# Third tiles at full width, an expert's number kept in a register, and another order of ScalarE's copies

## The chip, the cores and the metric

The kernel runs on one core of a Trainium2 chip. The metric is the device time of one execution in microseconds. Five engines run side by side, each taking its own instructions in order: TensorE (PE in the rows, PEld for its weight loads), VectorE (DVE), ScalarE (ACT), GpSimd (POOL) and SyncE (SP). Semaphores order them among each other. ACTq, POOLq and SPq in a row stand for an engine's queue issuing a transfer or another instruction that is not computing.

## The reference, cut to what matters

A mixture of experts on 4096 tokens of 256 values. Each token goes to the two of eight experts that its gate picks; the reference computes all eight and multiplies with a weight that is zero for six of them. Each expert is three dense layers, 256 to 512 to 512 to 256, and the weighted sum is added to the input.

```python
var = jnp.mean(x * x, axis=-1, keepdims=True)
xn = rms_w * (x * jax.lax.rsqrt(var + EPS))
gate_w = jax.nn.softmax(xn @ wg_W + wg_b + (genre_embed @ gg_W + gg_b), axis=-1)
topk_w, topk_i = jax.lax.top_k(gate_w, TOP_K)          # TOP_K = 2
cw = jnp.sum(jax.nn.one_hot(topk_i, E, dtype=x.dtype) * topk_w[..., None], axis=-2)
h1 = jax.nn.relu(jnp.einsum('bsh,ehm->bsem', x, W1) + b1)
h2 = jax.nn.relu(jnp.einsum('bsem,emn->bsen', h1, W2) + b2)
out_e = jnp.einsum('bsen,enh->bseh', h2, W3) + b3
return x + jnp.einsum('bseh,bse->bsh', out_e, cw)
```

## The kernel before

**Tiles and units.** The kernel computes the gate, sorts the tokens by expert into slots, and works through tiles of up to 128 slots of one expert. The first F = 7 tiles (one each of the experts 0 to 6) run singly while the rest of the sorting goes on. Behind them come *units* of one to four tiles of one expert. How many units of which width there are is a plan; the program holds a list of plans, of which a Switch picks one by the token counts at run time, so every plan's instructions are in the program and one set is executed. For these inputs it is the first of the table of shapes: five units of 512 columns, then units of 500, 480, 468, 448, 384, 352, 308 and 272 columns, then six pairs of 256. Units of 384, 352 and 308 columns have a third tile of 128, 96 and 52 columns; that of 272 has 16, for which 32 are computed.

**Layers 1 and 2.** `Fast(u, l)` computes layer l of unit u by a scheme of seven block products instead of eight. `p(k)` (L1178) are the products' matmuls, in fp32; `c11`, `c12`, `c22` and `c21` are VectorE's sums of products, `r1`, `r21`, `r2` and `r22` ScalarE's rectifiers (L1227), and `mix`, `fold` and `sum_of` VectorE's sums of the operands. A fp32 matmul of the program stands in the trace as two MATMUL records. Behind `p(1)`, `p(5)` and `p(6)` ScalarE copies a bank of PSUM: for a *seeded* unit (all but u = F) `p(1)`'s bank U is copied into bank A (L1187), and `p(2)` accumulates on it, so that the sum for c11 needs no VectorE; the other copies (L1189) go to SBUF. In a step, f = Fast(u, 0) is the first layer of unit u, g = Fast(u, 1) its second, and before = Fast(u - 1, 1) the second layer of the unit ahead.

**Layer 3.** Units of four tiles use `Wide`, the same scheme on the third layer. For units of three tiles that are followed by another of more than two, `Duo` takes the first two tiles by the scheme (L1356) and `third` (L1378) the last one by four plain matmuls on a bank that holds the bias. Duo's three banks are seeded by three copies on ScalarE (L1337, L1338, L1341): half of b3, a difference of its halves, and the whole for the third tile. All others use `layer3` (L1407). A third tile of at most 32 columns, here that of the 272-column unit, is computed by `parts_of` (L1431): the four k-tiles go to four groups of 32 columns of the array and so to four groups of 32 partitions; ScalarE copies these out (L1438), and `joined` (L1441) sums the four with a matmul against `quad`, four identities of 32 side by side.

**Weights.** `streams(u)` issues, on ScalarE's queue, the transfer of w1 for unit u + 2 (L1005), and of w2 (L1009) and w3 (L1013) for unit u + 1, into rings of buffers. Each first calls `expert(u, engine)`, which loads the unit's expert number from SBUF into a register of that engine (TENSOR_LOAD, L992). `scaled` (the bias times the gate weight) and Duo call it too.

**What sets the order.** The steps are written out by hand: an engine's instructions stand in the order in which `step_fast` and its neighbours call them, each engine's queue by itself. Around the change these are the step of u = F, the first unit with tiles that are computed together; that of u = CUT - 1 = F + 2, where `streams` was called ahead of `f.p(1)`; the steps behind a unit of three tiles (`duo(u)`); and the step behind the 272-column unit. The results of a tile go through `give` (VectorE, L1453) and `send` (GpSimd scatters rows, L1467).

Of the kernel before, what the change touches and what calls it, by code (L numbers as in the profile page):

```python
# [54 lines left out]
def kernel(  # L55
# [138 lines left out]
    both = const.tile([P, P // 2], F32, name="both")  # L194
    nc.gpsimd.tensor_tensor(both, ident[:, 0 : P // 2], ident[:, P // 2 : P], ALU.add)
    quad = const.tile([P, SQ], F32, name="quad")
    nc.gpsimd.tensor_tensor(quad, both[:, 0:SQ], both[:, SQ : 2 * SQ], ALU.add)
# [791 lines left out]

    def expert(u, engine):  # L990
        b = tiles(u)[0]
        _, (e,) = nc.values_load_multi_w_load_instructions(  # L992
            ebt[b - F : b - F + 1, 0:1],
            engines=[engine],
            min_val=0,
            max_val=E - 1,
            skip_runtime_bounds_check_because="a count of E - 1 comparisons",
        )
        return bass.ds(e, 1)
# [96 lines left out]
    class Fast:  # L1096
# [94 lines left out]
        def c11(self):  # L1191
# [4 lines left out]
            V.tensor_tensor(self.dst(0, 0), self.tall(self.A), self.q[0], ALU.add)  # L1196
# [32 lines left out]
        def r1(self):  # L1229
            for n in range(HB):  # L1230
                x = hid[self.l][:, n, self.w * self.seeded : 2 * self.w]
                self.relu(n, x, x)
# [91 lines left out]
    class Duo(Wide):  # L1324


        def __init__(self, u):
# [8 lines left out]
            self.b3 = b3_sb[:, e].rearrange("p e h -> p (e h)")  # L1336
            nc.scalar.copy(self.U, self.b3[:, 0 : H // 2])  # L1337
            nc.scalar.copy(self.X, b3d[:, e].rearrange("p e h -> p (e h)"))  # L1338
            if size(u) > 2:
                n = rows(u, 2)  # L1340
                nc.scalar.copy(self.last[0:n], self.b3[0:n])  # L1341
# [32 lines left out]
        def third(self):  # L1374
            cols, w3 = within(self.u, 2), ww[self.u][3]
            n = cols.stop - cols.start
            for c in range(MC):
                nc.tensor.matmul(  # L1378
                    self.last[0:n],
                    lhsT=hid[1][:, c, cols],  # L1380
# [21 lines left out]
    def layer3(u, which=None, order=range(MC)):  # L1402
        w3 = ww[u][3]
        for k in which or range(size(u)):
            for i, n in enumerate(order):
                cols = within(u, k)
                nc.tensor.matmul(  # L1407
                    sums(u, k)[0 : cols.stop - cols.start], lhsT=hid[1][:, n, cols], rhs=w3[:, n, :], start=(i == 0), stop=(i == MC - 1)
# [12 lines left out]

    def narrow(u, k):
        return size(u) == 3 and k == 2 and rows(u, k) <= SQ

    def parts_of(u, k):

        w3, n = ww[u][3], SQ
        cols, apart = slice(k * BT, k * BT + n), P // n
        for c in range(MC):
            q = c % apart  # L1430
            nc.tensor.matmul(  # L1431
                sums(u, k)[q * n : q * n + n],
                lhsT=hid[1][:, c, cols],
                rhs=w3[:, c, :],
                start=(c < apart),
                stop=(c >= MC - apart),
            )
        nc.scalar.copy(y_of(u, k), sums(u, k))  # L1438

    def joined(u, k):  # L1440
        nc.tensor.matmul(sums(u, k)[0:SQ], lhsT=quad, rhs=y_of(u, k), start=True, stop=True)  # L1441
# [195 lines left out]
    def step_fast(u, last):  # L1637
# [29 lines left out]
        if u == F:  # L1667
# [16 lines left out]
            f.c21()  # L1684
            f.r2()
# [8 lines left out]
        elif size(u - 1) == SLOTS:  # L1694
            before, third = Fast(u - 1, 1), Wide(u - 1)
            scales(u - 1)
            if u == CUT - 1:
                streams(u, last)
            f.p(1)
# [61 lines left out]
        elif duo(u):  # L1761
            before = Fast(u - 1, 1)
            scales(u - 1)
            f.p(1)
            before.c22()
            before.r22()
# [4 lines left out]
            pair = Duo(u - 1)  # L1771
# [49 lines left out]
        else:  # L1821
# [26 lines left out]
            thin = [k for k in last_ if narrow(u - 1, k)]  # L1848
            for k in thin:
                parts_of(u - 1, k)  # L1850
# [18 lines left out]
            for k in thin:  # L1869
                joined(u - 1, k)  # L1870
            if last_ and not thin:
                layer3(u - 1, last_)
# [10 lines left out]
        for k in (1, 5, 6, 2):  # L1883
            g.p(k)
# [63 lines left out]
    kept = (ww, ex, cgs, given, opened)  # L1948
# [42 lines left out]
```

## Time and profile before

| | us |
|---|---|
| median of 3 runs (lowest to highest) | 446.66 (446.6 to 446.8) |
| the profiled execution | 446.09 |
| its span, first to last instruction | 444.4 |

Stages of the span, with what the engines were busy in them (one row for each stretch, start:end, length, then busy us and number of instructions of the engines, the granted clock of TensorE, the share of the transfer engines and what they moved):

```
0.00:60.00 60.00, PE 58.68 (x501) PEld 52.86 (x502) DVE 51.84 (x217) ACT 38.73 (x102) POOL 34.44 (x47), clock 1.00, DMA 0.99, 351 GB/s
60.00:79.00 19.00, PE 19.00 (x148) PEld 18.36 (x147) DVE 8.21 (x24) ACT 8.78 (x24) POOL 10.17 (x10), clock 1.00, DMA 0.93, 299 GB/s
79.00:125.00 46.00, PE 45.55 (x236) PEld 39.52 (x235) DVE 39.28 (x88) ACT 21.57 (x48) POOL 36.43 (x29), clock 1.00, DMA 0.93, 267 GB/s
125.00:305.00 180.00, PE 180.00 (x1093) PEld 170.28 (x1092) DVE 144.80 (x326) ACT 100.96 (x245) POOL 119.14 (x91), clock 1.00, DMA 0.68, 176 GB/s
305.00:366.00 61.00, PE 60.99 (x444) PEld 57.42 (x443) DVE 48.57 (x133) ACT 36.80 (x115) POOL 38.75 (x31), clock 1.00, DMA 0.77, 207 GB/s
366.00:440.00 74.00, PE 73.10 (x563) PEld 70.09 (x562) DVE 53.02 (x142) ACT 42.03 (x131) POOL 36.82 (x28), clock 1.00, DMA 0.66, 180 GB/s
```

Up to 60 us are the gate, the sorting and the first single tiles; unit F's first and second layers lie between 79 and 100, unit F + 2's first products at 118; 305 to 366 holds the three-tile units and the one of 272 columns; behind it come the pairs. In a timeline a row is: start in us, length, engine, line and operation, tile written <- tiles read, shape, number of like instructions in the row, and in brackets how long the engine had been idle before it and what ended that. For a matmul, 128*52 128x256 is a weight block of 128 rows by 52 columns and 256 columns that move through it. Matmuls overlap, so a row's length is longer than the distance from its start to the next one.

### The profile page before, as it was taken

The numbers are of one execution on the slowest core, as the hardware profiler recorded it, in microseconds if no ns is written. First come the engines' busy times: TensorE is split into PE (matmuls) and PEld (weight loads), VectorE is DVE, ScalarE is ACT, GpSimd is POOL, SyncE is SP. The second block draws the span as 40 slices with busy tenths as digits, with TensorE's granted clock in tenths as the row PEclk, the third lists the DMA queues.
The fourth block names the chain that finished last, engine by engine and source line by source line (L and its number), as shares of the span: only waits on it lengthen the run. The fifth ranks groups of instructions, "written<-read, shape, count | busy, mean of one in ns | idle before, by whom it ended". The sixth has DMA issues, their size and how long they took to land. (4 is left out here: it accounts for less than half of the span.)

```text
span 444.4 us, 9217 instructions
## 1 busy us (share of the span) xinstructions
PE 437.3 (98%) x2975; PEld 408.5 (92%) x2975; DVE 345.7 (78%) x926; ACT 248.9 (56%) x662; POOL 276.8 (62%) x233
## 2 busy tenths in 40 slices
PE   9999999999999999999999999999999999999995
PEld 8699999789888999989999999999999989999994
DVE  6899964797869787786869697977977967778752
ACT  5855734537273645555464646466566565655562
POOL 6856244778878757484848483848757466674323
PEclk9999999999999999999999999999999999999999
DMA  8999998999995576475949493849669687799512
GB/s 309 318 366 389 357 358 294 282 298 257 234 301 116 136 219 158 136 194 130 242 115 239 98 247 80 253 101 240 176 173 265 199 238 204 230 281 263 167 18 47
DMA packets 85902, 96.98 MB, mean 218 GB/s; under 512 B 36079, under 2 KB 64850, under 8 KB 85716
## 3 DMA queue, kind: packets, MB, share of 16 engines
q1 hardware_dynamic: 49472, 40.54, 28.8%
q10 hardware_dynamic: 21188, 38.29, 26.9%
q0 software_dynamic: 15184, 17.47, 19.9%
q8 instruction: 25, 0.41, 0.4%
q14 instruction: 33, 0.27, 0.2%
HBM read 80.68 MB, written 20.20 MB: 227 GB/s over the span
## 5 line engine op out<-in xcount | busy, mean ns | idle before, releaser
L1467 POOL DMA_INDIRECT out_dram<-ys,idxR x60 | 99.1, 1652 | 90.7 <-DVE ys L1453 46.5
L895 POOL DMA_INDIRECT cg<-cwdR,idxR x60 | 65.9, 1099 | 18.3 <-issue 15.5
L1227 ACT ACTIVATE hid<-pb,bb 128x128 f32<-128x128 f32 (+9 forms) x146 | 51.7, 415 | 42.9 <-PE pb L1178 25.3
L1227 ACT ACTIVATE hid<-hid,bb 128x128 f32<-128x128 f32 (+10 forms) x154 | 62.4, 455 | 19.9 <-DVE hid L1202 6.5
L1178 PE MATMUL pb<-hid,w2r 128*128 128x128 f32 (+9 forms) x304 | 56.3, 328 | 0.0
L1178 PE MATMUL pb<-hotA,big 128*128 128x128 f32 (+9 forms) x304 | 53.6, 328 | 0.1
L1178 PEld LDWEIGHTS pb<-hotA,big 128*128 128x128 f32 x304 | 47.7, 191 | 3.6 <-ACT big L1189 0.5
L1178 PEld LDWEIGHTS pb<-hid,w2r 128*128 128x128 f32 x304 | 47.5, 191 | 3.3 <-ACT hid L1227 0.6
L895 POOL DMA_INDIRECT xgE<-in_x_dram,idxR x32 | 36.5, 1139 | 18.2 <-issue 8.8
L1178 PE MATMUL pb<-mixX,iotx 128*128 128x128 f32 (+9 forms) x228 | 46.4, 327 | 0.0
L1178 PEld LDWEIGHTS pb<-mixX,iotx 128*128 128x128 f32 x228 | 37.0, 191 | 2.2
L1407 PE MATMUL pb<-w3r,hid 128*128 128x256 f32 x160 | 37.9, 380 | 0.0
L1187 ACT COPY pb<-pb 128x256 f32<-128x256 f32 (+9 forms) x36 | 16.5, 459 | 37.1 <-PE pb L1178 31.4
L895 POOL DMA_INDIRECT big<-in_x_dram,idxR x28 | 31.7, 1131 | 8.5 <-issue 6.7
L1189 ACT COPY big<-pb 128x256 f32<-128x256 f32 (+9 forms) x39 | 18.8, 482 | 30.0 <-PE pb L1178 29.2
L1407 PEld LDWEIGHTS pb<-w3r,hid 128*128 128x128 f32 x160 | 29.0, 191 | 3.6 <-issue 0.4
L1178 PE MATMUL pb<-xT,w1r 128*128 128x128 f32 (+9 forms) x152 | 31.2, 327 | 0.3 <-ACT pb L1187 0.3
L950 DVE STREAM_TRANSPOSE xT<-gTs 128x256 f32<-128x256 f32 x56 | 29.6, 635 | 0.0
L1178 PE MATMUL pb<-mixB,w2r 128*128 128x128 f32 (+9 forms) x152 | 28.0, 327 | 0.0
L1178 PE MATMUL pb<-mixB,big 128*128 128x128 f32 (+9 forms) x152 | 28.0, 327 | 0.0
L1178 PE MATMUL pb<-hid,big 128*128 128x128 f32 (+9 forms) x152 | 28.0, 327 | 0.0
L1089 PE MATMUL pb<-hid,w2r 128*128 128x128 f32 x224 | 27.1, 276 | 0.0
(370 smaller groups left out, 954.8 us busy)
## 6 DMA issues: line engine op xcount, KB each, us to landing
w2r<-in_L_cond_W_dram ACTq DMA_DIRECT2D x17, 1024.0 KB, 7.6
w2r<-in_L_cond_W_dram SPq DMA_DIRECT2D x9, 1024.0 KB, 13.6
w3r<-in_L_cond_W_dram ACTq DMA_DIRECT2D x17, 512.0 KB, 10.1
w1r<-in_L_cond_W_dram ACTq DMA_DIRECT2D x16, 512.0 KB, 3.9
w1r<-in_L_cond_W_dram SPq DMA_DIRECT2D x10, 512.0 KB, 7.7
w3r<-in_L_cond_W_dram SPq DMA_DIRECT2D x9, 512.0 KB, 11.2
big<-in_x_dram SPq DMA_DIRECT2D x8, 512.0 KB, 6.3
gTs<-scr SPq DMA_DIRECT2D x8, 512.0 KB, 5.7
```

The costliest lines, as they stand in the source:

```text
L895: return nc.gpsimd.indirect_dma_start(out=dst, out_offset=None, in_=src, in_offset=bass.IndirectOffsetOnAxis(ap=index(b), axis=0), bounds_ ...
L950: V.transpose(xT[:, :, s0 + k, :].rearrange("p c (b k) -> p k c b", b=SQ), shs[:, s0 + k].rearrange("p k (a c) -> p k c a", a=SQ),)
L1089: nc.tensor.matmul(ph, lhsT=w2[:, m, ts(n, P)], rhs=hid[0][:, m, 0:BT], start=(m == 0), stop=(m == MC - 1))
L1178: nc.tensor.matmul(bank[:, ts(n, self.w)], lhsT=w[:, c, ts(n, P)], rhs=x[:, c], start=new and n == 0 and c == 0, stop=n == HB - 1 and c == ...
L1187: nc.scalar.copy(self.A, self.U)
L1189: nc.scalar.copy(self.q[(1, 6, 5).index(k)], self.tall(self.X if k == 5 else self.U))
L1227: nc.scalar.activation(out, src, AF.Relu, bias=ww[self.u][1][:, self.l, n : n + 1])
L1407: nc.tensor.matmul(sums(u, k)[0 : cols.stop - cols.start], lhsT=hid[1][:, n, cols], rhs=w3[:, n, :], start=(i == 0), stop=(i == MC - 1))
L1467: add = nc.gpsimd.indirect_dma_start(out=orows, out_offset=bass.IndirectOffsetOnAxis(ap=index(b)[0:n], axis=0), in_=y[0:n], in_offset=None ...
```

## The change

Seven edits, in the order of the program:

1. The tables `both` and `quad` and their two GpSimd instructions are dropped.
2. `expert` keeps the register it has loaded, by unit and engine, so a unit's number is loaded once on each engine. In the step of a unit, only w1's transfer (for u + 2) still brings a load; w2 and w3 (for u + 1), the scaling and Duo use what was loaded.
3. For an unseeded layer (unit F only) `c11` rectifies its half at once, in two pieces, and `r1` only the other half.
4. In the step of u = F, g's first product `p(1)`, with its copy on ScalarE, is called ahead of `f.r2()`.
5. In the steps behind a four-tile unit, `f.p(1)` is called ahead of `streams`, which concerns u = CUT - 1.
6. Duo's three seeding copies move to `seed`, called behind `before.c22()` and ahead of `before.r22()`. The last fills all 128 rows.
7. Third tiles are computed over 128 columns, the unused ones being stale and not sent; `narrow`, `parts_of` and `joined` are dropped, and `layer3` computes that tile where `joined` stood.

```diff
-    both = const.tile([P, P // 2], F32, name="both")
-    nc.gpsimd.tensor_tensor(both, ident[:, 0 : P // 2], ident[:, P // 2 : P], ALU.add)
-    quad = const.tile([P, SQ], F32, name="quad")
-    nc.gpsimd.tensor_tensor(quad, both[:, 0:SQ], both[:, SQ : 2 * SQ], ALU.add)
...
+    chosen = {}
+
     def expert(u, engine):
+        if (u, engine) in chosen:
+            return chosen[u, engine]
...
-        return bass.ds(e, 1)
+        chosen[u, engine] = bass.ds(e, 1)
+        return chosen[u, engine]
...
-            V.tensor_tensor(self.dst(0, 0), self.tall(self.A), self.q[0], ALU.add)
+            x = self.dst(0, 0)
+            V.tensor_tensor(x, self.tall(self.A), self.q[0], ALU.add)
+            for n in range(HB):
+                self.relu(n, x[:, n], x[:, n])
...
-                x = hid[self.l][:, n, self.w * self.seeded : 2 * self.w]
+                x = hid[self.l][:, n, self.w : 2 * self.w]
                 self.relu(n, x, x)
...
+            self.b3d = b3d[:, e].rearrange("p e h -> p (e h)")
+
+        def seed(self):
             nc.scalar.copy(self.U, self.b3[:, 0 : H // 2])
-            nc.scalar.copy(self.X, b3d[:, e].rearrange("p e h -> p (e h)"))
-            if size(u) > 2:
-                n = rows(u, 2)
-                nc.scalar.copy(self.last[0:n], self.b3[0:n])
+            nc.scalar.copy(self.X, self.b3d)
+            nc.scalar.copy(self.last, self.b3)
...
-                    self.last[0:n],
-                    lhsT=hid[1][:, c, cols],
+                    self.last,
+                    lhsT=hid[1][:, c, ts(2, BT)],
...
-    def parts_of(u, k):
-
-        w3, n = ww[u][3], SQ
-        cols, apart = slice(k * BT, k * BT + n), P // n
-        for c in range(MC):
-            q = c % apart
-            nc.tensor.matmul(
-                sums(u, k)[q * n : q * n + n],
-                lhsT=hid[1][:, c, cols],
-                rhs=w3[:, c, :],
-                start=(c < apart),
-                stop=(c >= MC - apart),
-            )
-        nc.scalar.copy(y_of(u, k), sums(u, k))
-
-    def joined(u, k):
-        nc.tensor.matmul(sums(u, k)[0:SQ], lhsT=quad, rhs=y_of(u, k), start=True, stop=True)
...
             f.c21()
+            g.p(1)
             f.r2()
...
+            f.p(1)
             if u == CUT - 1:
                 streams(u, last)
-            f.p(1)
...
+            pair = Duo(u - 1)
             f.p(1)
             before.c22()
+            pair.seed()
             before.r22()
             before.p(3)
             f.p(5)
             before.c12()
             before.r1()
-            pair = Duo(u - 1)
             pair.fold()
...
-            thin = [k for k in last_ if narrow(u - 1, k)]
-            for k in thin:
-                parts_of(u - 1, k)
...
-            for k in thin:
-                joined(u - 1, k)
-            if last_ and not thin:
+            if last_:
                 layer3(u - 1, last_)
...
-        for k in (1, 5, 6, 2):
+        for k in (5, 6, 2) if u == F else (1, 5, 6, 2):
             g.p(k)
```

Three places of ScalarE's queue show what moves. The names: `hid_93` and `hid_94` are the outputs of layer 1 and 2, `bb` the biases, `pb_68` to `pb_75` the eight banks of PSUM, `q1s` and `big` copies of products; lines of the changed kernel lie a few higher.

ScalarE in the step of u = F, before, from p(5)'s copy on:

```order
L1189 COPY q1s<-pb_69 128x512
L1189 COPY q1s<-pb_68 128x512
L1227 ACTIVATE hid_93<-hid_93,bb_1099 128x512 x2
L1227 ACTIVATE hid_93<-hid_93,bb_1099 128x256 x2
L1216 COPY q1s<-pb_71 128x512
L1575 DMA out_dram<-in_x_dram 128x1536
L1227 ACTIVATE hid_93<-hid_93,bb_1099 128x256 x2
L1189 COPY big<-pb_72 128x512
```

and of the change:

```order
L1231 ACTIVATE hid_93<-hid_93,bb_1089 128x256 x2
L1190 COPY q1s<-pb_69 128x512
L1190 COPY q1s<-pb_68 128x512
L1231 ACTIVATE hid_93<-hid_93,bb_1089 128x256 x4
L1220 COPY q1s<-pb_71 128x512
L1557 DMA out_dram<-in_x_dram 128x1536
L1190 COPY big<-pb_72 128x512
L1231 ACTIVATE hid_93<-hid_93,bb_1089 128x256 x2
```

Two rectifiers of 256 now stand ahead of p(5)'s copy, the pair of 512 has become one of 256 (the first two of the x4), and g.p(1)'s copy (big<-pb_72) stands ahead of r2's rectifiers.

ScalarE at the start of the step of u = F + 2, before (ISA rows set up a transfer):

```order
L992 TENSOR_LOAD ebt
L1005 ISA
L1005 DMA w1r_84<-in_L_cond_W_dram 128x1024
L992 TENSOR_LOAD ebt
L1009 ISA
L1009 DMA w2r_87<-in_L_cond_W_dram 128x4x512
L992 TENSOR_LOAD ebt
L1013 ISA
L1013 DMA w3r_90<-in_L_cond_W_dram 128x4x256
L1187 COPY pb_70<-pb_68 128x512
L1227 ACTIVATE hid_94<-hid_94,bb_1100 128x256 x2
L1189 COPY q1s<-pb_69 128x512
```

and of the change:

```order
L1188 COPY pb_70<-pb_68 128x512
L992 TENSOR_LOAD ebt
L1006 ISA
L1006 DMA w1r_84<-in_L_cond_W_dram 128x1024
L1010 ISA
L1010 DMA w2r_87<-in_L_cond_W_dram 128x4x512
L1014 ISA
L1014 DMA w3r_90<-in_L_cond_W_dram 128x4x256
L1231 ACTIVATE hid_94<-hid_94,bb_1089 128x256 x2
L1190 COPY q1s<-pb_69 128x512
```

p(1)'s copy has moved ahead of the three transfers, and two of their three loads are gone.

ScalarE in the step behind the 308-column unit, the third with Duo, before:

```order
L1187 COPY pb_70<-pb_68 128x272
L1227 ACTIVATE hid_94<-hid_94,bb_1098 128x154 x2
L1189 COPY q1s<-pb_69 128x272
L1227 ACTIVATE hid_94<-hid_94,bb_1098 128x154 x2
L992 TENSOR_LOAD ebt
L1337 ISA
L1337 COPY pb_73<-b_sb 128x128
L1338 ISA
L1338 COPY pb_74<-b3d 128x128
L1341 ISA
L1341 COPY pb_71<-b_sb 52x256
L1227 ACTIVATE hid_94<-pb_72,bb_1098 128x154 x2
```

and of the change:

```order
L1188 COPY pb_70<-pb_68 128x272
L1344 ISA
L1344 COPY pb_73<-b_sb 128x128
L1345 ISA
L1345 COPY pb_74<-b3d 128x128
L1346 ISA
L1346 COPY pb_71<-b_sb 128x256
L1231 ACTIVATE hid_94<-hid_94,bb_1088 128x154 x2
L1190 COPY q1s<-pb_69 128x272
L1231 ACTIVATE hid_94<-hid_94,bb_1088 128x154 x2
L1231 ACTIVATE hid_94<-pb_72,bb_1088 128x154 x2
```

The three seeds have moved from behind r1's rectifiers to ahead of r22's; r21's rectifiers (hid_94<-pb_72) now follow r1's directly, and a load is gone. TensorE's order is the same in both kernels except for the 272-column unit's third tile, and at u = F, where g.p(1) has the same place among TensorE's matmuls.

More of the change, by code (lines that the diff above doesn't have):

```diff
@@ L1374, in third @@
         def third(self):
-            cols, w3 = within(self.u, 2), ww[self.u][3]
-            n = cols.stop - cols.start
+            w3 = ww[self.u][3]
             for c in range(MC):
                 nc.tensor.matmul(
-                    self.last[0:n],
-                    lhsT=hid[1][:, c, cols],
+                    self.last,
+                    lhsT=hid[1][:, c, ts(2, BT)],
                     rhs=w3[:, c, :],
@@ L1405, in layer3 @@
             for i, n in enumerate(order):
-                cols = within(u, k)
                 nc.tensor.matmul(
-                    sums(u, k)[0 : cols.stop - cols.start], lhsT=hid[1][:, n, cols], rhs=w3[:, n, :], start=(i == 0), stop=(i == MC - 1)
+                    sums(u, k), lhsT=hid[1][:, n, ts(k, BT)], rhs=w3[:, n, :], start=(i == 0), stop=(i == MC - 1)
                 )
@@ L1420, in rows @@
         return cols.stop - cols.start
-    def narrow(u, k):
-        return size(u) == 3 and k == 2 and rows(u, k) <= SQ
-    def parts_of(u, k):
-        w3, n = ww[u][3], SQ
-        cols, apart = slice(k * BT, k * BT + n), P // n
-        for c in range(MC):
-            q = c % apart
-            nc.tensor.matmul(
-                sums(u, k)[q * n : q * n + n],
-                lhsT=hid[1][:, c, cols],
-                rhs=w3[:, c, :],
-                start=(c < apart),
-                stop=(c >= MC - apart),
-            )
-        nc.scalar.copy(y_of(u, k), sums(u, k))
-    def joined(u, k):
-        nc.tensor.matmul(sums(u, k)[0:SQ], lhsT=quad, rhs=y_of(u, k), start=True, stop=True)
     def give(u, which=None, summed=False, written=False, held=None):
@@ L1947 @@
             steps(u, u + 1, F + NQT + 1)
-    kept = (ww, ex, cgs, given, opened)
+    kept = (ww, ex, cgs, given, opened, chosen)
     state = [{k: list(v) if isinstance(v, list) else v for k, v in d.items()} for d in kept]
```

## The prediction, made before the changed kernel ran

> **What bounds the kernel.** First the page's busy shares and the clock, then the timeline of the end:
>
> ```profile
> PE 437.3 (98%) x2975; PEld 408.5 (92%) x2975; DVE 345.7 (78%) x926; ACT 248.9 (56%) x662; POOL 276.8 (62%) x233
> core 0: 444.4 us, clock 0.999
> 439.14 0.48 DVE L1453 SCALAR_TENSOR_TENSOR ys<-pb,cw,bc 128x256 f32<-128x256 f32 x1 [0.49 <-PE pb L1407]
> ```
>
> TensorE is busy for 98% of the span at full clock, and VectorE's last work waits for its last matmul; behind 439.62 there is only the last scatter. So time goes only where TensorE has less to do or stands still less. Its busy share hides standing still, since a matmul that waits is recorded as a longer one. I therefore read starts: in an undisturbed stretch of 256 columns the rows of 4 and 8 matmuls below (1.03, 1.89) give 0.86 for four, so 0.2158 from start to start and 0.38 for one alone. With 128 columns it is 0.112, and 0.61 for four. Whatever lies between two starts beyond that is lost. Each term below is such a loss, or a change in TensorE's own work; a gain ahead of 439 is kept as long as TensorE stays the last one.
>
> **Unit F+2, ScalarE's copy behind the weight transfers.**
>
> ```profile
> 118.52 1.03 PE L1178 MATMUL pb<-xT,w1r 128*128 128x256 f32 x4
> 121.97 1.89 PE L1178 MATMUL pb<-mixB,w2r 128*128 128x256 f32 x8
> 124.19 0.70 PE L1178 MATMUL pb<-xT,w1r 128*128 128x256 f32 x2 [0.33 <-ACT pb L1187]
> ```
>
> ```profile
> 121.13 0.42 ACTq L1005 DMA_DIRECT2D w1r<-in_L_cond_W_dram  x1
> 123.57 0.57 ACT L1187 COPY pb<-pb 128x512 f32<-128x512 f32 x1 [5.68 <-issue]
> ```
>
> Eight matmuls from 121.97 end their turn 2.22 later instead of 1.73, 0.49 lost; the pair at 124.19 takes 0.70 instead of 0.60, another 0.10. They are p(2), which accumulates on the bank that the copy at 123.57 seeds. Its source p(1) was done at 119.55, but ScalarE, which runs its instructions in order, stood 5.68 us at the three transfers, the first of which could not be issued before 121.13. The change puts the copy first: it fits from 119.6 to 120.2, ahead of 121.13, so the transfers keep their times and p(2) has its seed four microseconds early. Next late for p(2) would be its own operands, and 123.7, when it is due, is past all that the rows show late. **Gain 0.60**; nothing if the copy waited for something else, and the price of late weights is rival 4.
>
> **Unit F, rectifiers and copies.**
>
> ```profile
> 82.12 1.11 PE L1178 MATMUL pb<-xT,iotx 128*128 128x256 f32 x4
> 84.84 2.17 PE L1178 MATMUL pb<-hid,w2r 128*128 128x256 f32 x8
> 86.85 2.92 PE L1178 MATMUL pb<-hotA,big 128*128 128x256 f32 x11
> ```
>
> ```profile
> 81.45 0.59 ACT L1189 COPY q1s<-pb 128x512 f32<-128x512 f32 x1 [2.20 <-PE pb L1178]
> 84.06 1.33 ACT L1227 ACTIVATE hid<-hid,bb 128x512 f32<-128x512 f32 x2 [1.16 <-DVE hid L1199]
> 87.42 0.91 ACT L1227 ACTIVATE hid<-hid,bb 128x256 f32<-128x256 f32 x2 [0.76 <-DVE hid L1219]
> 88.23 1.13 ACT L1189 COPY big<-pb 128x512 f32<-128x512 f32 x2
> 80.07 0.68 DVE L1196 TENSOR_TENSOR hid<-pb,q1s 128x512 f32<-128x512 f32 x1
> ```
>
> From 82.12 to 84.84 twelve matmuls take 2.72 instead of 2.59: 0.08 in the first row (1.11 instead of 1.03: p(3) waits for the copy of 81.45) and 0.05 in front of g.p(1). The eight of g.p(1) take 2.01 to the next start instead of 1.73, 0.28 more; they read what the two rectifiers of 84.06 write. So g.p(1) loses 0.33. After the change half of that is rectified at 81 and the rest in two 256-wide pieces (0.45 each, as the row at 87.42 has them), done by 84.96, well before the second four of g.p(1). In the last row 11 matmuls take 2.92 instead of 2.54: p(6) loses 0.38 to the copy at 88.23, which stands behind two rectifiers that waited for VectorE until 87.42, though g.p(1) ended about 86.9. Moved ahead, it is done at 87.5. Against it: VectorE's sum (80.07, 0.68) ends at 80.75, the two new rectifiers take 0.91 behind it, and the next instruction overlaps them by 0.1 (88.23 against 87.42 + 0.91), so the copy of 81.45 starts at 81.6, 0.15 late, and p(3), already waiting for it, too. 0.33 + 0.38 - 0.15: **gain 0.56.** If the copy still came first it would be 0.71; if the rectifiers took 1.33, as today's pair of 512 does, p(3) would lose 0.57 and 0.14 would remain. I take the pair of 256, which has the size of the new one.
> The same split in the second layer puts 0.9 us of rectifiers in front of the next unit's first copy, which its p(2) needs. At F+2 5.7 us lie between the starts of p(1) and p(2) (118.52, 124.19), and the order is the same, so other products hide it: 0. Without that cover it would cost 0.9.
>
> **The seeds of Duo**, three copies in each of three steps:
>
> ```profile
> 343.78 0.63 PE L1178 MATMUL pb<-xT,iotx 128*128 128x136 f32 x4
> 344.39 0.71 PE L1356 MATMUL pb<-graw,hotA 128*128 128x128 f32 x4
> 344.94 0.68 PE L1356 MATMUL pb<-cw8B,hotA 128*128 128x128 f32 x4
> 328.76 0.70 PE L1356 MATMUL pb<-cw8B,hotA 128*128 128x128 f32 x4
> ```
>
> ```profile
> 341.56 0.39 ACT L1189 COPY q1s<-pb 128x272 f32<-128x272 f32 x1 [0.49 <-PE pb L1178]
> 342.48 0.26 ACT L1337 COPY pb<-b_sb 128x128 f32 x1
> 343.17 1.18 ACT L1227 ACTIVATE hid<-pb,bb 128x154 f32<-128x154 f32 x4
> ```
>
> Four matmuls of 136 columns should take 0.475 (0.112 by 136/128); the first row has 0.61 to the next start, 0.135 lost. Then 0.55 instead of 0.45, and 0.68 instead of 0.61: in all 0.31. The second Duo loses 0.09 (0.70 instead of 0.61). What they wait for comes through the rectifiers of 343.17, which follow the seeds (342.48 to 343.17, 0.69) without a gap. Moved ahead of r22 the seeds use the 0.49 that ScalarE stood idle before 341.56, so about 0.4 to 0.5 is won ahead of 343.17, more than the 0.31 lost. The price: r22 comes 0.69 later and the copy of 341.56 0.2 later (0.69 less the idle 0.49). The matmuls that overwrite what this copy reads are not due before the seeds' old place, so I charge nothing; without that slack it is 0.2 in each of three Duos, 0.6. **Gain 0.40**, bounds -0.2 and 0.40. That the last seed now fills 128 rows costs nothing, a copy's time going by its 256 columns (the gap from 342.48 to 343.17 is that of three copies one after the other).
>
> **The third tiles.** 52 columns become 128:
>
> ```profile
> 346.82 0.61 PE L1356 MATMUL pb<-w3r,mixB 128*128 128x128 f32 x4
> 347.36 1.93 PE L1378 MATMUL pb<-w3r,hid 128*52 128x256 f32 x8
> 349.22 0.73 PE L1178 MATMUL pb<-mixX,w1r 128*128 128x136 f32 x4
> ```
>
> Into the narrow weights 0.54 instead of 0.45, out of them 1.86 instead of 1.73, and 0.73 instead of 0.63: **gain 0.33**, since a matmul's time goes by the 256 columns that move. The 32-column tile, four column groups side by side and then one joining matmul (two records), becomes eight plain ones:
>
> ```profile
> 360.68 0.61 PE L1178 MATMUL pb<-mixX,iotx 128*128 128x128 f32 x4
> 361.22 0.64 PE L1431 MATMUL pb<-w3r,hid 128*32 128x256 f32 x8
> 361.79 0.70 PE L1407 MATMUL pb<-w3r,hid 128*128 128x256 f32 x2
> 363.62 0.61 PE L1178 MATMUL pb<-mixX,w1r 128*128 128x128 f32 x4
> 364.15 0.62 PE L1441 MATMUL pb<-ys,quad 128*32 128x256 f32 x2
> 364.70 0.49 PE L1178 MATMUL pb<-hid,w2r 128*128 128x128 f32 x2
> ```
>
> Beside it ScalarE loses one copy, which no row of TensorE waits for. The packed part costs 0.09 on entry, 0.57, and 0.10 on leaving; the joining one 0.08, 0.55 and 0.11: 1.51 together, against 8 x 0.2158 = 1.73. **Loss 0.22.** This is where a rule speaks against the change: the Trainium skill, "TensorE: Matmul & The Clock Gate", Part 3: Packing small matmuls, says that column tiles run at the same time, a span of about one matmul. The trace agrees for the packed part alone (0.57 for eight). An estimate by that rule, two passes and the joining two at 0.2158 each, is 0.86, so that unpacking would lose 0.87 and the forecast would be 445.05. I go by the rows, where the edges of about 0.1 are what costs. The Trainium skill's "TensorEngine Tiling (Array Packing)", Key Properties, says that changing the tiling mode drains the engine, which agrees with them.
>
> **The register loads.** An expert's number was loaded before each of three transfers; two of the three loads go.
>
> ```profile
> L992 ACTq TENSOR_LOAD <-ebt x68: 277/286/1187, 104.8 to 424.6; - x68
> 334.06 0.38 ACTq L1013 DMA_DIRECT2D w3r<-in_L_cond_W_dram  x1
> 334.49 0.67 ACT L1227 ACTIVATE hid<-pb,bb 128x154 f32<-128x154 f32 x2 [2.34 <-PE pb L1178]
> 335.43 1.62 PE L1178 MATMUL pb<-hotA,big 128*128 128x154 f32 x9
> 390.46 0.38 ACTq L1013 DMA_DIRECT2D w3r<-in_L_cond_W_dram  x1
> 390.89 0.69 ACT L1227 ACTIVATE hid<-hid,bb 128x128 f32<-128x128 f32 x2 [2.98 <-DVE ys L1453]
> 391.81 1.32 PE L1178 MATMUL pb<-hotA,big 128*128 128x128 f32 x8
> ```
>
> At 335.43 nine matmuls of 154 columns need 8 x 0.130 + 0.294 = 1.33 and took 1.62; at 391.81 eight need 1.06 and took 1.32. Lost: 0.28 and 0.26. In both places ScalarE's rectifiers start 0.05 after the last weight transfer is issued. Two loads fewer at 0.286 bring them forward by 0.57, twice what TensorE lost. **Gain 0.54**; nothing if the transfers wait for their buffers anyway or if, at 390.89, VectorE's L1453 that the row names is the true releaser. Elsewhere loads lie beside idle ScalarE: 0. The two GpSimd sums for the removed tables end at 9 us, long before their use: 0.
>
> **The sum.** 0.60 + 0.56 + 0.40 + 0.33 - 0.22 + 0.54 = 2.2 us. The profiled run took 446.09 us (444.4 of span and 1.7 around it), so 443.9 in the same execution; it lies 0.57 under the median of the runs, 446.66, which gives **444.4**.
>
> **Rivals.** (1) The stalls go only in part: what comes next on ScalarE is hardly earlier. Then the register loads (0.54) and half of the seeds and of unit F (0.48) fail: 445.4. For it speaks that the row at 390.89 names VectorE, and that ScalarE's rows around 342 lie without gaps; against it, that ScalarE is busy for only 56% and that at F+2 the idle time is plainly its queue's. (2) The edges of 0.1 belong to their places in the program (operands that come late there) and not to the width. Then the 52-column tile gives nothing and the plain 32-column one keeps 0.38 of edges: 0.33 + 0.38 more, 445.1. Against it: three different neighbours show the same 0.1. (3) The change is made, but TensorE, earlier, meets weights or token rows that land no earlier. Then all that is won by standing still less (2.1) is waited away, and only its own work's 0.33 - 0.22 stays: 446.5. Against it: TensorE's rows here name ScalarE, never a transfer, as what they wait for. That the loads or the orders would not change at all is excluded by the instruction rows shown with the change. (4) Slower: at unit F+2 the copy now stands ahead of the weight transfers. If p(1) ended after 120.5 instead of 119.55, w1r, w2r and w3r would be issued late, and the fold of a late w2r holds its engine as it does once now:
>
> ```profile
> DVE big L1137 <- DMA w2r<-in_L_cond_W_dram: 3.3, 1, 3.3
> ```
>
> If all of that 3.3 reached TensorE, it would be 444.4 + 3.3 = 447.7. It decides from a delay of p(1) by 0.95 us, and TensorE comes there 0.56 earlier than before.
>
> **Chances.** Forecast 0.55, rival 1 0.20, rival 2 0.10, rival 3 0.11, slower 0.04. A difference of 0.2%, 0.9 us, is about what a measurement of this kernel can tell from no change; faster therefore holds below 445.8: 0.85, same 0.11, slower 0.04. The range goes from 443.6 (unit F without its 0.15, the highest instead of the median run's distance, and some small stalls that go with the loads) to 445.9, with rivals 1 and 2 inside and about half a microsecond beyond them.
>
> **What would show it.** In the changed profile the matmuls of p(2) at unit F+2, of g.p(1) and p(6) at unit F, and of both Duos should have starts 0.2158 (or their width's share) apart; the three weight transfers should be issued with one load ahead; no row of TensorE has 52 or 32 columns behind the gating. p(3) of unit F should be about 1.25. A forecast that is wrong would show as a new idle time before ScalarE's copies, as transfers of w1r after 121, or as matmuls that are late somewhere new.

## The result, and the profile after

| | before | after |
|---|---|---|
| median of 6 runs each, us (lowest to highest) | 446.73 (445.96 to 447.02) | 443.63 (443.39 to 445.48) |
| ratio of the runs, with its 95% interval | | 0.9939 (0.9922 to 0.9957) |
| profiled execution, us | 446.09 | 443.66 |
| its span, us | 444.4 | 441.9 |

The kernel became faster by 0.6%, 1.9 to 3.5 us by the interval. The forecast was 444.4, with a range from 443.6 to 445.9, so the median lies at its lower edge. The ratios, here and in the last series, are taken over the runs and not over the medians, and leave out runs of a slower state (two of the kernel before and two of the changed one in the last series).

The page, the view of the cores and VectorE's timeline at the end, after:

```profile
PE 435.5 (99%) x2973; PEld 410.3 (93%) x2973; DVE 345.4 (78%) x926; ACT 250.2 (57%) x665; POOL 275.3 (62%) x231
core 0: 441.9 us, clock 0.997
436.92 0.48 DVE L1435 SCALAR_TENSOR_TENSOR ys<-pb,cw,bc 128x256 f32<-128x256 f32 x1 [0.51 <-PE pb L1410]
```

TensorE is still the bound, at 99%. VectorE's last operation starts at 436.92 instead of 439.14, 2.22 earlier. The other 0.28 of the span lie behind it, where nothing was changed.

Since TensorE runs nearly the same matmuls in the same order, the start of each can be compared in the two traces, and the difference changes only where one of them stood still or did other work:

| place | predicted gain | gain in TensorE's starts |
|---|---|---|
| up to 80 us | 0 | 0.03 |
| unit F | 0.56 | 0.52 (-0.19 at p(3), 0.33 at g.p(1), 0.38 at p(6)) |
| unit F+2, p(2) | 0.60 | 0.60 |
| Duo, second and third | 0.40 | 0.42 |
| behind the transfers near 335 and 392 | 0.54 | 0.54 |
| third tile of 52 columns | 0.33 | 0.33 |
| third tile of 32 columns | -0.22 | -0.22 |
| together | 2.21 | 2.22 |

The timelines of the changed kernel at these places, in the order of the prediction. Unit F+2, TensorE and ScalarE:

```profile
121.63 1.67 PE L1179 MATMUL pb<-mixB,w2r 128*128 128x256 f32 x7
123.14 1.03 PE L1179 MATMUL pb<-xT,w1r 128*128 128x256 f32 x4
119.03 0.57 ACT L1188 COPY pb<-pb 128x512 f32<-128x512 f32 x1 [1.69 <-PE pb L1179]
120.16 0.42 ACTq L1006 DMA_DIRECT2D w1r<-in_L_cond_W_dram  x1
121.34 0.39 ACTq L1014 DMA_DIRECT2D w3r<-in_L_cond_W_dram  x1
```

Seven matmuls from 121.63 take 1.51 to the next start, 7 x 0.2158, and the four of 123.14 are 1.03 long: nothing is lost. The copy runs at 119.03, right behind p(1). But the first transfer is issued at 120.16, a microsecond earlier than before, of which only 0.55 is TensorE's gain up to here. In both traces its release is the landing of a store of SyncE (scr<-big, L934 before and L930 after: token rows on their way to a later unit), at 121.11 before and at 120.14 now. The two transfers that follow are issued within 1.18 instead of 1.90.

Unit F, TensorE, then ScalarE:

```profile
82.25 1.13 PE L1179 MATMUL pb<-xT,iotx 128*128 128x256 f32 x4
84.95 1.89 PE L1179 MATMUL pb<-hid,w2r 128*128 128x256 f32 x8
86.67 3.62 PE L1179 MATMUL pb<-hotA,big 128*128 128x256 f32 x16
80.82 0.91 ACT L1231 ACTIVATE hid<-hid,bb 128x256 f32<-128x256 f32 x2 [1.59 <-DVE hid L1198]
81.64 1.24 ACT L1190 COPY q1s<-pb 128x512 f32<-128x512 f32 x2
84.22 1.31 ACT L1231 ACTIVATE hid<-hid,bb 128x256 f32<-128x256 f32 x3 [1.34 <-DVE hid L1203]
86.87 0.59 ACT L1190 COPY big<-pb 128x512 f32<-128x512 f32 x1 [0.48 <-PE pb L1179]
87.36 0.91 ACT L1231 ACTIVATE hid<-hid,bb 128x256 f32<-128x256 f32 x2
```

g.p(1) takes 1.89, p(6) lies in an unbroken row of 16 (15 x 0.2158 + 0.38 = 3.62), and its copy runs at 86.87, ahead of r2. The price is there too: the two new rectifiers push p(5)'s copy from 81.45 to 81.64, and p(3) from 82.12 to 82.25 although TensorE came there 0.03 earlier; with another 0.02 between p(3)'s first two matmuls that is 0.19. Its row is 1.13 long and not the 1.25 that was expected, since the wait now lies ahead of its start.

The third Duo, TensorE and ScalarE, and behind it the third tiles of the 308- and the 272-column unit:

```profile
342.26 0.63 PE L1179 MATMUL pb<-xT,iotx 128*128 128x136 f32 x4
342.72 0.61 PE L1361 MATMUL pb<-graw,hotA 128*128 128x128 f32 x4
343.17 0.61 PE L1361 MATMUL pb<-cw8B,hotA 128*128 128x128 f32 x4
345.42 1.89 PE L1382 MATMUL pb<-w3r,hid 128*128 128x256 f32 x8
347.14 0.63 PE L1179 MATMUL pb<-mixX,w1r 128*128 128x136 f32 x4
358.95 1.89 PE L1410 MATMUL pb<-w3r,hid 128*128 128x256 f32 x8
340.15 0.37 ACT L1190 COPY q1s<-pb 128x272 f32<-128x272 f32 x1
341.09 1.20 ACT L1231 ACTIVATE hid<-pb,bb 128x154 f32<-128x154 f32 x4
```

Rows of four are 0.61 and 0.63 long again, without a gap between them, on both sides of the third tile too. The rectifiers that followed the seeds now start at 341.09, 1.17 ahead of TensorE's 342.26; before it was 0.61 (343.17 and 343.78).

The register loads and ScalarE behind the two transfers:

```profile
L992 ACTq TENSOR_LOAD <-ebt x19: 278/287/690, 104.2 to 397.8; - x19
332.37 0.67 ACT L1231 ACTIVATE hid<-pb,bb 128x154 f32<-128x154 f32 x2 [1.86 <-PE pb L1179]
387.22 0.73 ACT L1231 ACTIVATE hid<-hid,bb 128x128 f32<-128x128 f32 x2 [1.40 <-DVE hid L1206]
```

68 loads became 19. Both rectifiers now wait for their data, TensorE's products and VectorE's sum L1206 (before, the row of 390.89 named the L1453 that started at 390.23; its counterpart here, L1435, starts at 388.27, a microsecond behind the rectifiers, so they do not need it).

### The profile page after: what moved, and what is told of

Read it like the earlier page. It is cut to its first block, busy times and chain, and to the rows that moved or that the text cites. A ratio compares the mean times of both kernels' runs of the same rounds, so it can differ in the third digit from the quotient of the medians.

```text
span 441.9 us, 9156 instructions
## 1 busy us (share of the span) xinstructions
PE 435.5 (99%) x2973; PEld 410.3 (93%) x2973; DVE 345.4 (78%) x926; ACT 250.2 (57%) x665; POOL 275.3 (62%) x231
## 5 line engine op out<-in xcount | busy, mean ns | idle before, releaser
L1231 ACT ACTIVATE hid<-hid,bb 128x256 f32<-128x256 f32 (+9 forms) x158 | 63.5, 452 | 22.4 <-DVE hid L1206 8.5
L1410 PE MATMUL pb<-w3r,hid 128*128 128x256 f32 x168 | 39.7, 380 | 0.0
L891 POOL DMA_INDIRECT big<-in_x_dram,idxR x28 | 30.8, 1100 | 8.5 <-issue 7.0
L1410 PEld LDWEIGHTS pb<-w3r,hid 128*128 128x128 f32 x168 | 30.5, 191 | 3.3
```

What stands on the lines that cost most here:

```text
L891: return nc.gpsimd.indirect_dma_start(out=dst, out_offset=None, in_=src, in_offset=bass.IndirectOffsetOnAxis(ap=index(b), axis=0), bounds_ ...
L1231: nc.scalar.activation(out, src, AF.Relu, bias=ww[self.u][1][:, self.l, n : n + 1])
L1410: nc.tensor.matmul(sums(u, k), lhsT=hid[1][:, n, ts(k, BT)], rhs=w3[:, n, :], start=(i == 0), stop=(i == MC - 1))
```

## The experiments

A single time cannot tell a few tenths of a microsecond, so the runs that undo one part are read by TensorE's starts against those of the changed kernel; where they differ in the first 52 us, that difference is taken off. In the two series of these runs the kernel before, run once in each, took 448.05 and 446.83 us, so the single times below are not to be set against the 443.63 of the result.

**The loads back.**

```diff
     def expert(u, engine):
-        if (u, engine) in chosen:
-            return chosen[u, engine]
```

> The changed kernel with the register loads back (an expert's number is loaded before each use again); all else as changed. Read by TensorE's starts against the changed kernel's, since a single time spreads by more. Theory (the loads held the rectifiers behind the transfers): TensorE loses 0.28 in the 154-column products near 335 and 0.26 in the 128-column products near 390 again, 0.54 together, nothing elsewhere. Rival (those two stalls went with the other edits, or VectorE's sum was the true releaser): TensorE's starts stay as they are, under 0.1 in all.

It took 444.93 us. Behind 52 us TensorE lost 1.45: 0.22 and 0.36 at unit F+2, 0.37 near 350, 0.05 near 390 and 0.44 near 404. The view of that line, and timelines of TensorE and ScalarE:

```profile
L990 ACTq TENSOR_LOAD <-ebt x68: 278/286/1575, 104.0 to 423.7; - x68
124.77 1.13 PE L1177 MATMUL pb<-xT,iotx 128*128 128x256 f32 x4
127.78 1.16 PE L1302 MATMUL pb<-cw8B,hotA 128*128 128x128 f32 x8
403.02 1.06 PE L1177 MATMUL pb<-hotA,big 128*128 128x128 f32 x8
404.26 1.16 PE L1177 MATMUL pb<-hotA,big 128*128 128x128 f32 x8 [0.18 <-DVE mixB L1160]
400.11 0.38 ACTq L1008 DMA_DIRECT2D w2r<-in_L_cond_W_dram  x1
402.30 0.38 ACTq L1012 DMA_DIRECT2D w3r<-in_L_cond_W_dram  x1
402.73 0.70 ACT L1229 ACTIVATE hid<-hid,bb 128x128 f32<-128x128 f32 x2 [3.17 <-DMA w1r<-in_L_cond_W_dram]
```

The loads do cost TensorE time, more than expected, and not where they did in the first trace of before. Between the two transfers at 400.11 and 402.30 lies one load of 1.575 us, and the rectifiers stand behind it. The stall near 350 follows a load of 0.78 at 345.8; in the first trace of before the stalls near 335 and 392 followed loads of 0.57 at 332.4 and of 1.19 at 389.1. Slow loads without a stall exist too (0.89 at 154.2 in the first trace), so it takes a slow load at a place without slack. The rival falls as to loads in general, but 0.54 was what one execution drew. At unit F+2 no load was slow: three ordinary ones and the transfers between them held r22 and what follows, with p(1)'s copy already ahead of them, for 0.58. The first of these transfers also went out later than in any other run; the run with the transfers first, below, comes back to this.

**The seeds at their old place.**

```diff
             before.c22()
-            pair.seed()
             before.r22()
...
             before.r1()
+            pair.seed()
             pair.fold()
```

> The changed kernel with Duo's three seeding copies at their old place behind r1, without the load that stood ahead of them. Theory (the seeds delay r21's rectifiers and with them Duo's operands): the third Duo loses about 0.3 and the second about 0.1 again, 0.42 in all. Rival (it was the register load ahead of the seeds, gone by the other edit): under 0.1.

It took 444.23 us, and TensorE lost 0.12 at the second Duo and 0.28 at the third, 0.40. TensorE and ScalarE at the third:

```profile
342.41 0.63 PE L1179 MATMUL pb<-xT,iotx 128*128 128x136 f32 x4
342.98 0.71 PE L1361 MATMUL pb<-graw,hotA 128*128 128x128 f32 x4
343.53 0.68 PE L1361 MATMUL pb<-cw8B,hotA 128*128 128x128 f32 x4
341.80 1.19 ACT L1231 ACTIVATE hid<-pb,bb 128x154 f32<-128x154 f32 x4
```

These are the rows of before again, 0.10 each too long where Duo's products start; the rectifiers lead TensorE's 342.41 by 0.61 as they did before. The load had nothing to do with it: the place of the seeds is the cause.

**The transfers first at unit F+2**, with one load among them.

```diff
-            f.p(1)
             if u == CUT - 1:
                 streams(u, last)
+            f.p(1)
```

> The changed kernel with the weight transfers of unit F+2 ahead of p(1)'s copy again, but with one register load in them instead of three. Theory as predicted (the first transfer is held until about 120 to 121, whatever the loads): p(2) stalls again, by 0.6 less what two loads fewer save (0.35 each as transfers now follow one another 0.65 later instead of 0.95 to 1.0), so 0 to 0.1. Rival (the place in the queue alone decides): the whole 0.6.

It took 443.84 us. TensorE's starts did not change by 0.04 anywhere behind 52 us. ScalarE and TensorE:

```profile
119.95 0.42 ACTq L1006 DMA_DIRECT2D w1r<-in_L_cond_W_dram  x1
121.13 0.40 ACTq L1014 DMA_DIRECT2D w3r<-in_L_cond_W_dram  x1
121.57 0.57 ACT L1188 COPY pb<-pb 128x512 f32<-128x512 f32 x1 [3.94 <-PE pb L1179]
121.70 1.89 PE L1179 MATMUL pb<-mixB,w2r 128*128 128x256 f32 x8
123.43 1.03 PE L1179 MATMUL pb<-xT,w1r 128*128 128x256 f32 x4
```

The copy stands behind the transfers as in before, but with two loads fewer among them it runs at 121.57 instead of 123.57, and p(2) at 123.43 finds it done. The rival, that the place in the queue alone decides, falls: with the loads gone, the order is worth nothing here. But the loads are not all that differs from before: the first transfer went out 1.70 us behind p(1)'s start (118.25) here, and 2.61 behind it before. What it waits for is the store of SyncE named above, whose landing SyncE's next transfer (gTs<-scr) waits for as well. The two go out together; with the loads back, and in the run with the packed tile below:

```profile
121.03 0.42 ACTq L1004 DMA_DIRECT2D w1r<-in_L_cond_W_dram  x1
121.08 0.36 SPq L937 DMA_DIRECT2D gTs<-scr  x1
120.67 0.42 ACTq L1011 DMA_DIRECT2D w1r<-in_L_cond_W_dram  x1
120.72 0.36 SPq L942 DMA_DIRECT2D gTs<-scr  x1
```

| run | loads with the transfers | what stands first | first transfer behind p(1)'s start, us | lost at unit F+2, us |
|---|---|---|---|---|
| before | 3 | transfers | 2.61 | 0.60 |
| loads back | 3 | copy | 3.29 | 0.58 |
| transfers first | 1 | transfers | 1.70 | 0 |
| after | 1 | copy | 2.20 | 0 |
| 32-column tile packed | 1 | copy | 2.82 | 0 |
| the other five runs of these two series | 1 | copy | 1.56 to 2.37 | 0 |

So the moment moves by about a microsecond between executions with the same loads, and in the packed run it came later than before although the loads were gone: the loads of earlier steps are not shown to set it. An estimate from these rows: had the first transfer come 2.61 behind p(1) in this run too, 0.91 later, the copy would have ended 4.80 behind p(1)'s start, still ahead of the 5.18 at which p(2) is due. And with the loads back, all that stands behind the transfers would have been 0.68 earlier, more than the 0.48 by which TensorE's row at 127.78 was late there (10.04 behind p(1)'s start, 9.56 in the changed kernel). By this estimate either half of the change, two loads fewer or the copy first, was enough to win the 0.60, and the runs do not show how it is to be divided.

**g.p(1)'s copy behind r2 at unit F again.**

```diff
-            g.p(1)
             f.r2()
...
-        for k in (5, 6, 2) if u == F else (1, 5, 6, 2):
+        for k in (1, 5, 6, 2):
```

> The changed kernel with g.p(1)'s copy behind r2's rectifiers at unit F again. Theory: p(6) near 88 loses 0.38 again. Rival (p(6) waited for r2's rectifiers or the copy came late for another reason): under 0.1.

It took 443.35 us; p(6) lost 0.28. ScalarE and TensorE:

```profile
86.67 0.91 ACT L1231 ACTIVATE hid<-hid,bb 128x256 f32<-128x256 f32 x2 [0.76 <-DVE hid L1223]
87.49 1.22 ACT L1190 COPY big<-pb 128x512 f32<-128x512 f32 x2
86.20 3.47 PE L1179 MATMUL pb<-hotA,big 128*128 128x256 f32 x14
```

Fourteen matmuls take 3.47 where 3.19 are needed. The theory holds. The 0.10 of the 0.38 that did not come back can be read from the starts: against before, with the start of the run taken off, the copy (87.49 for 88.23) comes 0.23 earlier, and TensorE, by what unit F gains ahead of it, only 0.14.

**Unit F's rectifiers as before**, none behind c11 and r1 in two pieces of 512.

```diff
-            x = self.dst(0, 0)
-            V.tensor_tensor(x, self.tall(self.A), self.q[0], ALU.add)
-            for n in range(HB):
-                self.relu(n, x[:, n], x[:, n])
+            V.tensor_tensor(self.dst(0, 0), self.tall(self.A), self.q[0], ALU.add)
...
-                x = hid[self.l][:, n, self.w : 2 * self.w]
+                x = hid[self.l][:, n, self.w * self.seeded : 2 * self.w]
```

> The changed kernel with unit F's rectifiers as before: none behind c11, and r1 rectifies both halves in two 512-wide pieces. Read by TensorE's starts. Theory: g.p(1) near 85 loses 0.31 to 0.33 again, p(3) near 82 wins back the 0.13 that the change cost it, net 0.18 slower. Rival (the split changed nothing and g.p(1)'s stall went because its copy moved): p(3) wins 0.13 and nothing is lost.

It took 443.15 us. p(3) won 0.19 and g.p(1) lost 0.33, net 0.14 slower by the starts; the time is among the lowest for another reason, 0.45 that TensorE won ahead of 52 us. The split is worth what its term said, and its price is real.

**The two rectifiers where ScalarE is idle.** They go behind p(6)'s copy.

```diff
             V.tensor_tensor(x, self.tall(self.A), self.q[0], ALU.add)
+            if self.l:
+                self.r11()
+
+        def r11(self):
             for n in range(HB):
                 self.relu(n, x[:, n], x[:, n])
...
             f.p(6)
+            f.r11()
             f.p(3)
```

> The changed kernel with c11's two rectifiers of unit F behind p(6)'s copy instead of ahead of p(5)'s, where ScalarE stands idle. Theory (p(3) is late only because p(5)'s copy is): p(3) near 82 wins 0.13 and g.p(1) loses nothing. Rival (the rectifiers now delay r1's half): g.p(1) loses up to 0.3.

It took 443.36 us. ScalarE and TensorE:

```profile
81.42 0.58 ACT L1190 COPY q1s<-pb 128x512 f32<-128x512 f32 x1 [2.20 <-PE pb L1179]
82.76 0.91 ACT L1235 ACTIVATE hid<-hid,bb 128x256 f32<-128x256 f32 x2
82.08 1.11 PE L1179 MATMUL pb<-xT,iotx 128*128 128x256 f32 x4
```

p(5)'s copy is at its old place, p(3) starts 0.17 earlier than in the changed kernel and TensorE wins 0.19, the whole price; g.p(1) loses nothing. Only the 0.08 stays that p(3) lost in before (1.11 instead of 1.03).

**A third tile of 64 columns** in the 308-column unit.

```diff
-                    self.last,
-                    lhsT=hid[1][:, c, ts(2, BT)],
+                    self.last[0:64] if rows(self.u, 2) == 52 else self.last,
+                    lhsT=hid[1][:, c, slice(2 * BT, 2 * BT + 64) if rows(self.u, 2) == 52 else ts(2, BT)],
```

> The changed kernel with the third tile of the 308-column unit computed over 64 columns instead of 128 (52 are used). Theory (a weight block of at most half the array's columns switches TensorE into another tiling): about 0.33 lost around 345 to 347, as with 52 columns before. Rival A (only an odd number such as 52 costs): 0. Rival B (the edges belong to the place in the program): 0 in the starts, as the changed kernel shows none there.

It took 444.13 us, 0.34 lost by TensorE's starts:

```profile
345.17 0.61 PE L1361 MATMUL pb<-w3r,mixB 128*128 128x128 f32 x4
345.71 1.94 PE L1382 MATMUL pb<-w3r,hid 128*64 128x256 f32 x8
347.58 0.73 PE L1179 MATMUL pb<-mixX,w1r 128*128 128x136 f32 x4
```

The edges of before are back (345.17 to 345.71 is 0.54 instead of 0.45, the eight take 1.87 instead of 1.73, and 0.73 instead of 0.63 behind them). Neither the number 52 nor the place makes them: 64 columns do, and 128 at the same place do not. Nor did the 96 columns of the 352-column unit in before, whose eight matmuls took 1.73 like those of 128 in the changed kernel. The Trainium skill ("TensorEngine Tiling (Array Packing)", Tiling Modes) lists a tiling of 64 columns and says that a change of the tiling mode drains the engine. That would fit; no row shows the mode itself.

**The 32-column tile packed again**, with its joining matmul and tables as in the kernel before.

```diff
+            thin = [k for k in last_ if narrow(u - 1, k)]
+            for k in thin:
+                parts_of(u - 1, k)
...
+            for k in thin:
+                joined(u - 1, k)
-            if last_:
+            if last_ and not thin:
                 layer3(u - 1, last_)
```

> The changed kernel with the 272-column unit's third tile packed into four column groups again, with the joining matmul and its tables. Theory: 0.22 faster than the changed kernel between 358 and 363 (1.51 instead of 1.73). Rival (the packed form's edges came from late operands, which are earlier now): 0.3 to 0.6 faster.

It took 443.35 us. Between 358 and 363 TensorE won 0.22 against the changed kernel, as the term said; the rival's 0.3 to 0.6 falls. Dropping the packing is the one part of the change that costs.

**A last series** held the changed kernel with the first and third of these edits together (loads back, transfers first), the two kernels themselves, and the changed kernel with the two edits that won together (rectifiers behind p(6)'s copy, packed tile).

> The changed kernel with the register loads back and, at unit F+2, the transfers ahead of p(1)'s copy: both halves of what stood there before. In the runs with one half alone the stall of 0.60 at p(2) was absent (order back: 0) or smaller and elsewhere (loads back: 0.25 near 125). Theory (either half is enough to bring the copy in time): with both back p(2) near 123 loses about 0.6 again. Rival (another edit, such as unit F's, moved the first transfer forward): under 0.2 there. Elsewhere the loads cost something between 0.5 and 1.3, by where a slow one falls.

> The kernel before, unchanged, another execution. Question: is the half microsecond by which its runs differ, and by which the gain of the medians (3.1) is more than the 2.2 of TensorE's starts, in the loads? Theory (some of its register loads take 0.5 to 1.6 us instead of 0.29, and which ones differs from run to run): against the first trace of before, stalls behind weight transfers come and go by 0.2 to 0.5 each, and before 60 us the starts shift by up to 0.6. Rival (all runs have the same stalls and only what lies behind the last matmul differs): TensorE's starts agree within 0.1 behind 60 us.

> The changed kernel, unchanged, in five rounds beside the kernel before. Theory: 2.2 us of TensorE's work and waiting, and something more since its 19 loads on ScalarE leave less to chance than 68: ratio 0.992 to 0.995, and a smaller spread of its runs than before's. Rival (the first measurement was lucky): 0.996 or more.

> The changed kernel with the two edits that each won something by themselves: c11's rectifiers of unit F behind p(6)'s copy (0.13), and the 32-column third tile packed (0.22). Theory: they lie in different places and add, 0.35 us less than the changed kernel by TensorE's starts, a ratio to before about 0.0008 lower than the changed kernel's, which these rounds hardly tell from none. Rival: the packed tile's copy on ScalarE delays something at its place, and 0.13 or less remains.

| | median, us | runs | ratio to before |
|---|---|---|---|
| before | 463.46 | 23 | |
| loads and order back | 460.73 | 1 | |
| before, its own trace | 465.31 | 1 | |
| after | 461.86 | 12 | 0.9954 (0.9920 to 0.9989) |
| rectifiers behind, and packed | 460.98 | 12 | 0.9943 (0.9911 to 0.9975) |

In this series every kernel, that of before too, took 4% longer. In its traces engines stood still for several microseconds at a time, released by something that the trace does not name ("remote"), so that only the ratios and stretches without such pauses can be read. ScalarE, TensorE, and a window of the kernel before there (the windows' last figures are TensorE's granted clock, the share of the transfer engines, and GB/s):

```profile
75.64 1.14 ACT L1092 ACTIVATE hid<-pb,vT 128x128 f32<-128x128 f32 x4 [7.53 <-remote]
76.06 3.60 PE L1077 MATMUL pb<-xT,w1r 128*128 128x128 f32 x16 [4.47 <-ACT hid L1092]
76.00:80.00 4.00, 3.94 (x19) 3.89 (x20) 0.15 (x1) 2.12 (x8) 0.00 (x0) 0.58 0.75 214
```

The changed kernel's gain repeats, since its interval ends below 1. Its 0.9954 lies between the 0.995 of the theory and the 0.996 of the rival, and its runs spread as much as before's (457.95 to 467.31 against 460.88 to 470.0), so the smaller spread that was expected did not come. At unit F+2 nothing was lost with both halves back, against the 0.6 expected, and nothing in the kernel before either: the first transfer went out at 129.06 in the former, 0.94 before p(1) started (130.00), and held nobody. So the same loads in the same order cost 0.60 in one execution and nothing in another, by when the first transfer goes out; how loads and order share the 0.60 stays open. The combined kernel won 0.22 by its packed tile in TensorE's starts; unit F could not be compared. Its ratio is 0.0011 lower than the changed kernel's, with intervals that overlap almost wholly: that it is the fastest is what its parts say, not what its times show. The rival that all executions have the same stalls falls, as the kernel before lost 0.60 at unit F+2 in one and nothing there in another; but the pauses keep this from showing that the loads make the half microsecond between runs.

## Why the prediction was right, and where its reasons were not

**The sum** was right to 0.01 us in TensorE's starts (2.21 against 2.22), and each term to 0.04, because each was a loss that the trace already held. That it fits to a hundredth is luck: 0.03 of it arose at the start of the run, and unit F gave 0.04 less than its term. The medians moved by 3.1, the profiled pair by 2.4. The forecast lay 0.8 above the median, and its gain of 2.2 within the measurement's interval of 1.9 to 3.5. The profiled execution of before was 0.6 under its median; that others had more slow loads would fit, but this was not shown.

**Unit F+2: the size right, the cause not the order's alone.** The step was that p(1)'s copy behind the transfers is the loss, and that moving it first wins 0.60 while "the transfers keep their times". That the late copy held p(2) is what the rows of before show. But with two loads fewer the old order lost nothing, so the 0.60 cannot be put down to the order alone; and with the loads back the new order lost 0.58 at what follows r22, which also stands behind the transfers. I had followed only the first instruction behind the queue's long stay, not the next ones, and had not asked what releases the first transfer. It is the landing of SyncE's store, which came between 1.70 and 3.29 us behind p(1)'s start wherever it held the queue in the first two series, and before p(1) in the last one. Nor did the transfers keep their times: three with two loads fewer are issued within 1.2 instead of 1.9 us, so that a load costs the queue 0.36, not the 0.29 of its own length.

**The register loads: right in sum, too certain.** 0.54 was two stalls of one execution. The runs showed a cost that changes with where slow loads fall: 0.87 in the run with the loads back outside unit F+2, and 0.58 there, in an execution whose first transfer was also the latest. The rows near 390 leave no ground for the doubt of rival 1 (that VectorE's L1453 was the releaser): its counterpart in the changed kernel starts at 388.27, and the rectifiers at 387.22.

**Duo's seeds**: mechanism and size right; 0.40 comes back with the place alone. Nothing stalled on p(5)'s copy, as assumed; it comes 0.1 later against TensorE (340.15 for 341.56, where TensorE is 1.52 earlier), not 0.2.

**Unit F**: right. The pair of 256 was the right row for the two new rectifiers; p(3) lost 0.19, the term had 0.15, and the whole gave 0.52 for 0.56. That the price was avoidable (0.19 back with the rectifiers behind p(6)'s copy) could have been read from ScalarE's 1.16 of idle time ahead of 84.06.

**The third tiles**: right, both. The packed form's rows gave the loss of 0.22, and the estimate by the rule of packing (0.87) would have put it four times too high, since entering, leaving and joining cost 0.93 of the 1.16 that the concurrent matmuls save (1.73 less 0.57).

**The rivals.** Rival 1 falls, since every stall that was priced went. Rival 2 falls by the 64 columns, which bring the edges back at a place that has none with 128. Nothing of rival 3 was seen: no wait of TensorE on a transfer appeared that was not there before. Rival 4 did not occur: p(1) ended at 119.0, and the first transfer went out behind its copy, 1.0 earlier than before.

## What to carry to other kernels

Where an engine is busy for 98%, look at starts, not at busy time: a stall is hidden in a longer record, and can be priced before it is removed (here each term came within 0.04 us). When a queue is held, ask what releases its first instruction and follow everything that stands behind it; moving one instruction ahead only helps if the next one has slack, and shortening what holds the queue helps all of them. Two edits can each be enough for the same stall, and then undoing one of them shows nothing. A single tile of 52 or 64 columns between full ones paid about 0.33 us here and one of 96 nothing, so fill such a tile up; four groups of 32 side by side still won 0.22.

## What the runs showed of the hardware that had not been expected

- A register load from SBUF on ScalarE's queue takes 0.28 us as a rule and up to 1.6 at times (0.69, 1.19 and 1.58 were the longest in three executions), at other places in each execution.
- The first 128-column matmuls start 0.21 us apart and later ones 0.11, and the change from one to the other came at another moment in each execution: eight such matmuls from 4.70 took 1.06 in one run and 1.94 from 4.73 in another. This shifts all that follows by up to 0.8 us between runs of kernels that are alike there. The Trainium skill, "TensorE: Matmul & The Clock Gate", Part 1: The HAM clock gate, has the cause as a window of activity that runs freely, so that the moment varies by half a microsecond either way. In the runs here it varied by more, from about 4.3 us to past 6.2, and the granted clock of the profile reads 1.00 on both sides of it, so that they do not show the cause.
- After TensorE had stood for 4.5 us in the last series, 16 matmuls of 128 columns took 3.60 instead of about 1.95 (15 x 0.112 + 0.27), at a granted clock of 0.58 in that window.
